# Row transforms in column pairs, a different order of the last loads, and a separated normalisation in a transformer block followed by a Fourier block

## The chip, the cores and the metric

The kernel runs on one core of one Trainium2 chip. The metric is the device time of one execution in microseconds (us); the number given is the median of several runs. A core has five engines with queues of their own: TensorE (matmuls, PE in the profile; its weight loads are PEld), VectorE (DVE), ScalarE (ACT), GpSimd (POOL) and SyncE (SP, used here only to issue DMAs). SBUF is the on-chip memory of 128 partitions, PSUM the accumulators that matmuls write, and DRAM the memory off the core.

## The reference

The input is an image of 48 x 48 tokens with 768 channels. Layer 0 is a transformer block: layer norm, 12-head attention with relative positions, a projection, and then

```python
xn2 = layernorm(x, ln2_g, ln2_b)
h = jax.nn.gelu(xn2 @ mlp_w1 + mlp_b1, approximate=False)
return x + (h @ mlp_w2 + mlp_b2)
```

Layer 1 is a Fourier block. It transforms the image in both directions, multiplies every kept frequency by two small complex layers (8 blocks of 96 channels), shrinks, transforms back and adds its input:

```python
xf = jnp.fft.rfft2(x.astype(jnp.float32), axes=(1, 2), norm='ortho')
...
y = jnp.fft.irfft2(z.reshape(B, H, Wh, C), s=(H, W), axes=(1, 2), norm='ortho')
return y.astype(x.dtype) + bias
```

All is float32. A row of 48 tokens has 25 frequencies (KW), each with a real and an imaginary part, so 50 numbers per row and channel.

## The kernel before

The 2304 tokens lie in 18 tiles of 128 partitions, x1[:, t, :], in SBUF for the whole second part of the kernel. The two edges of a 128-token tile cut rows of 48 tokens: three tiles hold 8 whole rows. Nearly all large products are made by a scheme of seven half-size products instead of eight, whose sums are made by VectorE and GpSimd.

**MLP.** It runs over three blocks p of 768 tokens (six tiles), and in each over 12 steps n of 256 hidden features. A step has hidden(p, n) in three pieces (matmuls into the PSUM banks h0 to h3, L989; VectorE sums u and c, L1001; ScalarE's gelu, L995; VectorE's sums hs, L154 to L157), and between the pieces added(p, n - 1, i) for i = 0, 1, 2, the product of the step before with the second weight matrix: seven matmuls into the banks o0 to o3, each bank emptied by VectorE into x1 or acc (L1049 to L1057). Three of the four banks are used twice within one added, so the second use waits for the first eviction.

The next block's tokens must be normalised before the block begins. normalised(p + 1, i) is written in the program in steps 4 to 9; it calls normalise (L116 to L124: two statistics, an aggregate, ScalarE's square root, a reciprocal and the tensor_scalar that writes the tile hat), and GpSimd then adds the bias b2 to x1. The order of the program holds only for TensorE here: inside manual_schedule TensorE keeps the written order, and the other engines' instructions are placed by a scheduler, which moves an instruction ahead when its inputs and its buffer are there. So the tokens of block 1 are normalised at the very beginning of block 0, and those of block 2 in the turn from block 0 to block 1. turned (L1104, L1105) transposes the six hats at the block's end.

**Forward row transform.** rows_forward(p), after each block, multiplies the block's 16 rows by the row DFT, for each half k of the channels (384 each) and each group g of three tiles (eight rows). A group gives 8 x 50 = 400 outputs, in four PSUM tiles zp of 100 partitions (two rows). Since tile edges cut rows, two of the four tiles need two matmuls: six of 128 x 100 by 384 (L1076) per group. ScalarE (or both, in the last block) copies zp to zt, and SP writes zt to DRAM, z1[k].

**Fourier part.** 14 units (7 per half, four frequencies each, the last of each half only one) go through four stages, each one round r later than the one before: columns (L1202), first (L1221 to L1238), second (L1252 to L1261) and back (yp, L1271), whose output y goes to z2 in DRAM. In a round TensorE's order is, for i = 0 to 3: back, second, first, columns, and from round 12 on one piece of the first half's inverse row transform.

**Inverse row transform.** rows_back(half, g) loads a 100 x 4 x 384 tile zo (600 KB) from z2, and makes three output tiles, each of two matmuls (rps, L1292); VectorE adds x1 (yt, L1295) and SP writes the result. zo has three buffers and yt four. In the function pieces the generators run one after the other: each load is written just ahead of its own matmuls, and the buffers decide how early it can be issued. All loads and writes are issued by SP, in one order. The second half's loads depend on the last unit's y.

## Time and profile before

| | |
|---|---|
| median of 3 runs | 2929.87 us (2922.76 to 2933.12) |
| the profiled execution's own time | 2924.9 us |
| its span, first to last instruction | 2922.9 us, TensorE clock 0.998 |
| TensorE busy | 2864.6 us (98%) |
| VectorE, ScalarE, GpSimd busy | 1791.0, 936.3, 609.8 us |
| MLP with forward row transforms | from 1625 to 2672 us |
| Fourier part and inverse row transform | from 2672 us to the end |

In a group's line of the profile, the numbers after x are the count of instructions, and after the bar the busy time in us, the mean duration of one in ns, and the idle time of the engine just before them with what ended it. In a timeline's line they are the start, the duration of the merged run, the engine, the line of the kernel, the tile written and the tiles read, the array shape of a matmul as rows x columns in use (128*100), and in brackets the idle time before. A line of the waits gives the total in us, the number of times, and the longest. A line of the chain gives start and duration of one link of the work that ended last. A float32 matmul of the program appears as two records.

### The profile page before, as it was taken

Reading aid. Unit: us, or ns where it says so; the run is one execution under the profiler, and the core shown is the slowest. Engines: PE = TensorE matmul, PEld = TensorE weight load, DVE = VectorE, ACT = ScalarE, POOL = GpSimd, SP = SyncE. Lnnn points to the kernel's source line nnn. Section 1 sums busy time; section 2 is a strip of 40 time slices with the busy share of each in tenths; the row PEclk is TensorE's granted clock in tenths of the full one; section 3 lists DMA queues with packets and bytes.
Section 4 is the critical chain, followed back from the end, with each engine's and each line's share of the span. In section 5 each row is a group of like instructions: output and inputs, shape, how many; then the busy total and the mean of one; then the engine's idle time right before and its main releaser. Section 6 shows DMA issues by size and latency. Waiting matters only on the chain. (4 is left out here: it accounts for less than half of the span.)

```text
span 2922.9 us, 40961 instructions
## 1 busy us (share of the span) xinstructions
PE 2864.6 (98%) x15659; PEld 1724.2 (59%) x15659; DVE 1791.0 (61%) x2606; ACT 936.3 (32%) x1514; POOL 609.8 (21%) x564
## 2 busy tenths in 40 slices
PE   7999999999999999999999999999999999999998
PEld 4555665555555555555555555555555555556885
DVE  5243237777777777777733666674666566665564
ACT  1011126656666565665500211122011211102331
POOL 2302110000000000000043322343332323222441
PEclk9999999999999999999999999999999999999999
DMA  3423276173462716435252111212121212113235
GB/s 127 148 88 118 92 162 123 30 135 64 82 128 41 144 34 101 109 59 87 56 177 76 43 56 53 65 64 65 57 65 54 77 54 65 54 57 99 79 93 179
DMA packets 202818, 253.03 MB, mean 87 GB/s; under 512 B 21618, under 2 KB 180978, under 8 KB 201078
## 3 DMA queue, kind: packets, MB, share of 16 engines
q1 hardware_dynamic: 202614, 250.32, 33.5%
q8 instruction: 126, 2.06, 0.3%
q14 instruction: 78, 0.64, 0.1%
HBM read 136.40 MB, written 50.14 MB: 64 GB/s over the span
## 5 line engine op out<-in xcount | busy, mean ns | idle before, releaser
L635 DVE TENSOR_TENSOR acc<-acc,main 128x768 f32<-128x768 f32 x576 | 551.9, 958 | 206.4 <-ACT main L569 149.9
L569 ACT ACTIVATE main<-sp 128x768 f32<-128x768 f32 x648 | 520.8, 812 | 138.9 <-PE sp L565 132.2
L565 PE MATMUL sp<-terms,select 64*128 64x384 f32 x1296 | 413.3, 630 | 0.0
L1051 DVE TENSOR_TENSOR main<-o,main 128x384 f32<-128x384 f32 x540 | 299.4, 557 | 40.3 <-PE o L1049 2.1
L989 PE MATMUL h<-shared,w 128*128 128x384 f32 x864 | 296.7, 486 | 0.8 <-issue 0.8
L559 PE MATMUL sp<-shared 64*128 64x384 f32 x1296 | 268.0, 490 | 2.5 <-DVE o L457 2.2
L559 PE MATMUL sp<-qT,kT 64*128 64x384 f32 x1296 | 266.7, 487 | 0.2
L612 POOL TENSOR_TENSOR inverse<-inverse,rden 128x384 f32<-128x384 f32 x36 | 46.3, 1287 | 1010.7 <-DVE rden L609 918.1
L446 PE MATMUL m<-main 128*128 128x384 f32 x756 | 247.0, 488 | 6.4 <-DVE rstd L121 3.0
L989 PEld LDWEIGHTS h<-shared,w 128*128 128x128 f32 x864 | 164.4, 190 | 116.1 <-issue 2.3
L989 PE MATMUL h<-shared,w1s 128*128 128x384 f32 x648 | 226.6, 486 | 0.0
L582 PE MATMUL op<-main,shared 128*64 128x384 f32 x1296 | 221.2, 488 | 0.0
L582 PE MATMUL op<-main,v 128*64 128x384 f32 x1296 | 219.9, 488 | 0.0
L995 ACT ACTIVATE hT<-c,vec 128x384 f32<-128x384 f32 x108 | 66.4, 615 | 466.2 <-DVE c L1001 466.1
L446 PEld LDWEIGHTS m<-main 128*128 128x128 f32 x756 | 142.6, 190 | 108.3 <-issue 8.7
L1001 DVE TENSOR_TENSOR c<-h,u 128x384 f32<-128x384 f32 x108 | 60.2, 557 | 212.3 <-PE h L989 212.3
L1049 PE MATMUL o<-w,hT 128*128 128x384 f32 x432 | 175.0, 487 | 3.0 <-DVE mv L118 2.0
L1049 PE MATMUL o<-w2s,hs 128*128 128x384 f32 x432 | 174.8, 487 | 3.1 <-DVE hs L155 3.1
L565 PEld LDWEIGHTS sp<-terms,select 64*128 64x128 f32 x1296 | 125.8, 187 | 83.9 <-issue 0.5
L989 PEld LDWEIGHTS h<-shared,w1s 128*128 128x128 f32 x648 | 123.1, 190 | 85.9
L154 POOL TENSOR_TENSOR w1s<-w 128x384 f32<-128x384 f32 x36 | 36.4, 1010 | 610.9 <-PE o L1049 289.4
L559 PEld LDWEIGHTS sp<-shared 64*128 64x128 f32 x1296 | 117.9, 187 | 61.3 <-issue 23.1
(158 smaller groups left out, 3896.8 us busy)
## 6 DMA issues: line engine op xcount, KB each, us to landing
w<-in_mlp_w_dram SPq DMA_DIRECT2D x72, 768.0 KB
terms<-col_parts SPq DMA_DIRECT2D x432, 72.0 KB
terms<-row_hi SPq DMA_DIRECT2D x216, 72.0 KB
terms<-row_lo SPq DMA_DIRECT2D x216, 72.0 KB
main<-in_qkv_w_dram SPq DMA_DIRECT2D x36, 384.0 KB
z<-zt SPq DMA_DIRECT2D x48, 150.0 KB
zo<-z SPq DMA_DIRECT2D x12, 600.0 KB
x<-in_x_dram SPq DMA_DIRECT2D x18, 384.0 KB
```

The costliest lines, as they stand in the source:

```text
L446: nc.tensor.matmul(bank, a[:, c, :], b[:, c, :], start=(first and c == 0), stop=(c == 2), skip_group_check=not first,)
L559: nc.tensor.matmul(sp[:, j, :G], kT[at, ts(kt, P)], qT[at, ts(c, G)], start=True, stop=False,)
L565: nc.tensor.matmul(sp[:, j, :G], select[at, a % 2], ready[pr, c][at, a // 2, b], start=False, stop=True,)
L569: nc.scalar.activation(p, sp[:, :, :G], AF.Exp, scale=HD**-0.5)
L582: nc.tensor.matmul(op[ts(j, 64)], v[:, kt0 + i, ts(j, 64)], ps[i][:, j, :], start=(kt0 + i == 0), stop=(kt0 + i == NT - 1),)
L612: nc.gpsimd.tensor_tensor(inverse, inverse, rden, ALU.add)
L635: nc.vector.tensor_tensor(acc, made[0] if kt == 1 else acc, p, ALU.add)
L989: nc.tensor.matmul(bank[i], a[:, c, :], b[:, c, :], start=(start and c == 0), stop=(c == 2), skip_group_check=not start,)
L995: nc.scalar.activation(h[:, i, ts(k, G)], src, AF.Gelu, bias=col(V_B1 + 2 * n + i))
L1001: nc.vector.tensor_tensor(t, src, other, ALU.add)
L1049: nc.tensor.matmul(bank[k], a, b, start=start, stop=True, skip_group_check=not start)
L1051: nc.vector.tensor_tensor(dst, bank[k], dst, ALU.add)
```

## The change

It has three parts.

1. **Rows in pairs.** In both row transforms a matmul now covers one row (64 columns of the array, 50 of them in use in the forward direction) and goes to one half of a PSUM tile's partitions; two such matmuls with different halves stand next to each other. The forward transform pads a row's 50 outputs to 64, so z1 has 64 rows per image row, zp and zt have 128 partitions, and a group takes ten matmuls of 64 columns in five pairs. The inverse writes half a tile's outputs (64 partitions) per matmul, eight in four pairs per group; its three PSUM tiles take the tags f, m and l, which the units use too. The four zt tiles of a group become slices of one tile with two buffers.
2. **Loads.** in_turn takes the place of pieces: the first half's loads run three ahead and the second half's four ahead; four of the twelve zo tiles take buffers of zt, which is free by then; the second half's loads are issued by ScalarE. The first half's pieces now stand in the rounds 13 to 16, three in each, instead of 12 to 16.
3. **Normalisation.** It is split into measured (statistics, steps 3 to 8; after the last, one square root and one reciprocal for all six tiles) and normalised (the tensor_scalar and GpSimd's addition, two tiles in each of steps 9 to 11). pinned keeps these instructions in the written order relative to their engine's other work.

```diff
-    z1 = [dram.tile([HW * 2 * KW, CH], F32, name=f"z1_{k}") for k in range(2)]
+    z1 = [dram.tile([HW * 64, CH], F32, name=f"z1_{k}") for k in range(2)]
...
-        rows = z1[half].rearrange("(r k) c -> r k c", k=KW)
+        rows = z1[half].rearrange("(r k) c -> r k c", k=32)
...
-        rows_dft = bias.tile([P, 6, 2 * 2 * KW], F32, name="rows_dft")
+        rows_dft = bias.tile([P, 3, 8, 64], F32, name="rows_dft")
...
-                    for a, parts in enumerate(((0,), (1, 2), (3, 4), (5,))):
-                        zp = psum.tile([2 * 2 * KW, CH], F32, name="zp", tag=f"o{a}")
-                        for b in parts:
+                    zp = []
+                    for pair in (((0, 0), (0, 1)), ((0, 2), (1, 3)), ((1, 2), (1, 5)),
+                                 ((1, 4), (2, 5)), ((2, 6), (2, 7))):
+                        for i, r in pair:
+                            if r // 2 == len(zp):
+                                zp.append(psum.tile([P, CH], F32, name="zp", tag=f"o{len(zp)}"))
                             nc.tensor.matmul(
-                                zp, rows_dft[:, b, :], x1[:, 3 * g + b // 2, ts(k, CH)],
-                                start=(b == parts[0]), stop=(b == parts[-1]),
+                                zp[r // 2][ts(r % 2, 64)], rows_dft[:, i, r],
+                                x1[:, 3 * g + i, ts(k, CH)],
+                                start=((i, r) not in ((1, 2), (2, 5))),
+                                stop=((i, r) not in ((0, 2), (1, 5))), skip_group_check=True,
                             )
-                        zt = turn.tile([2 * 2 * KW, CH], F32, name="zt", bufs=8)
+                    zt4 = turn.tile([P, 4, CH], F32, name="zt", bufs=2)
+                    for a in range(4):
+                        zt = zt4[:, a]
                         if p < 2:
-                            nc.scalar.copy(zt, zp)
+                            nc.scalar.copy(zt, zp[a])
                         else:
-                            balanced_copy(a, zt, zp)
-                        nc.sync.dma_start(out=z1[k][ts(4 * g + a, 4 * KW), :], in_=zt)
+                            balanced_copy(a, zt, zp[a])
+                        nc.sync.dma_start(out=z1[k][ts(4 * g + a, P), :], in_=zt)
...
+        moments = bias.tile([P, 6, 2], F32, name="moments")
+        rstd6 = bias.tile([P, 6], F32, name="rstd6")
+        pinned = tc.keep_in_program_order
+
+        def measured(p, i):
+
+            stats = upool.tile([P, 2, 6], F32, name="stats")
+            for j in range(2):
+                pinned(nc.vector.bn_stats(stats[:, j, :], x1[:, 6 * p + i, ts(j, C // 2)]))
+            pinned(nc.vector.bn_aggr(moments[:, i], stats.rearrange("p a b -> p (a b)")))
+            if i == 5:
+                pinned(nc.scalar.activation(rstd6, moments[:, :, 1], AF.Sqrt, bias=eps))
+                pinned(nc.vector.reciprocal(rstd6, rstd6))
+
         def normalised(p, i):
-
             t = 6 * p + i
             hats[i] = turn.tile([P, C], F32, name="hat2", tag="turn")
-            normalise(upool, x1[:, t, :], hats[i])
+            pinned(
+                nc.vector.tensor_scalar(
+                    hats[i], x1[:, t, :], moments[:, i, 0:1], rstd6[:, i : i + 1],
+                    ALU.subtract, ALU.mult,
+                )
+            )
             nc.gpsimd.tensor_tensor(x1[:, t, :], x1[:, t, :], b2, ALU.add)
...
-                    if p < 2 and 4 <= n < 10:
-                        normalised(p + 1, n - 4)
+                    if p < 2 and 3 <= n < 9:
+                        measured(p + 1, n - 3)
+                    elif p < 2 and n >= 9:
+                        for i in range(2):
+                            normalised(p + 1, 2 * (n - 9) + i)
...
-            zo = zin.tile([4 * KW, 4, CH], F32, name="zo", bufs=3)
-            nc.sync.dma_start(
+            if (T // G * half + g) % 5 in (1, 3):
+                zo = turn.tile([P, 4, CH], F32, name="zo2", tag="zt", bufs=2)[: 4 * KW]
+            else:
+                zo = zin.tile([4 * KW, 4, CH], F32, name="zo", bufs=3)
+            (nc.scalar if half else nc.sync).dma_start(
                 out=zo, in_=z2[half][ts(g, 16 * KW), :].rearrange("(a p) c -> p a c", a=4)
             )
             yield
-            for i in range(3):
-                yt = mid.tile([P, CH], F32, name="yt", bufs=4)
-                rp = psum.tile([P, CH], F32, name="rps", tag="f")
-                for e in range(2):
+            rp = []
+            for a, pair in enumerate(
+                (((0, 0), (0, 1)), ((1, 0), (0, 1)), ((2, 0), (1, 1)), ((2, 0), (2, 1)))
+            ):
+                if a < 3:
+                    rp.append(psum.tile([P, CH], F32, name="rps", tag="fml"[a]))
+                for i, j in pair:
+                    shared_half = (i, j) in ((0, 1), (2, 0))
                     nc.tensor.matmul(
-                        rp, irows[:, 2 * i + e, :], zo[:, i + e, :], start=(e == 0), stop=(e == 1)
+                        rp[i][ts(j, 64)], irows[:, a + i, ts(j, 64)], zo[:, a, :],
+                        start=(not shared_half or a % 2 == 0),
+                        stop=(not shared_half or a % 2 == 1), skip_group_check=shared_half,
                     )
-                nc.vector.tensor_tensor(yt, rp, x1[:, 3 * g + i, ts(half, CH)], ALU.add)
+                if a == 0:
+                    continue
+                i = a - 1
+                yt = mid.tile([P, CH], F32, name="yt", bufs=4)
+                nc.vector.tensor_tensor(yt, rp[i], x1[:, 3 * g + i, ts(half, CH)], ALU.add)
                 nc.sync.dma_start(out=out[ts(3 * g + i, P), ts(half, CH)], in_=yt)
                 yield
...
-        def pieces(gens):
-            for gen in gens:
-                yield from gen
+        def in_turn(gens, ahead):
+
+            for gen in gens[:ahead]:
+                next(gen)
+            yield
+            for g, gen in enumerate(gens):
+                for _ in range(3):
+                    next(gen)
+                    yield
+                for gen in gens[g + ahead : g + ahead + 1]:
+                    next(gen)
...
-            first_half = pieces(ends[0])
+            first_half, second_half = in_turn(ends[0], 3), in_turn(ends[1], 4)
...
-                    if r > len(units) // 2 + 4:
-                        next(first_half, None)
+                    if (r, i) == (len(units) - 2, 3) or (r > len(units) - 2 and i < 3):
+                        next(first_half)
+            next(second_half)
             for _ in first_half:
                 pass
-            for _ in pieces(ends[1]):
+            for _ in second_half:
                 pass
```

The tables that the host makes for rows_dft change their layout with it; the numbers in them are the same, with zeros in the padding.

More of the change, by code (lines that the diff above doesn't have):

```diff
@@ L1287, in rows_back @@
             yield
-            for i in range(3):
-                yt = mid.tile([P, CH], F32, name="yt", bufs=4)
-                rp = psum.tile([P, CH], F32, name="rps", tag="f")
-                for e in range(2):
-                    nc.tensor.matmul(
-                        rp, irows[:, 2 * i + e, :], zo[:, i + e, :], start=(e == 0), stop=(e == 1)
-                    )
-                nc.vector.tensor_tensor(yt, rp, x1[:, 3 * g + i, ts(half, CH)], ALU.add)
+            rp = []
[6 more added lines that the diff above has]
+                    shared_half = (i, j) in ((0, 1), (2, 0))
+                    nc.tensor.matmul(
+                        rp[i][ts(j, 64)], irows[:, a + i, ts(j, 64)], zo[:, a, :],
+                        start=(not shared_half or a % 2 == 0),
+                        stop=(not shared_half or a % 2 == 1), skip_group_check=shared_half,
+                    )
+                if a == 0:
+                    continue
+                i = a - 1
+                yt = mid.tile([P, CH], F32, name="yt", bufs=4)
+                nc.vector.tensor_tensor(yt, rp[i], x1[:, 3 * g + i, ts(half, CH)], ALU.add)
                 nc.sync.dma_start(out=out[ts(3 * g + i, P), ts(half, CH)], in_=yt)
@@ L1340, in _constants @@
             select[32 + 16 * part + w, :, :, w] = 1.0
-    fr = np.stack([cos[:, :KW], -sin[:, :KW]], 1).reshape(n, 2 * KW)
+    fr = np.zeros((n, 2, 32))
+    fr[:, 0, :KW], fr[:, 1, :KW] = cos[:, :KW], -sin[:, :KW]
     twice = np.full((KW, 1), 2.0)
@@ L1349, in _constants @@
     ir = np.concatenate([cos[:KW] * twice, -si], 0)
-    fwd = np.zeros((8 * n, 8 * 2 * KW))
+    fwd = np.zeros((8 * n, 8, 64))
     inv = np.zeros((8 * 2 * KW, 8 * n))
     for r in range(8):
-        fwd[r * n : (r + 1) * n, r * 2 * KW : (r + 1) * 2 * KW] = fr
+        fwd[r * n : (r + 1) * n, r] = fr.reshape(n, 64)
         inv[r * 2 * KW : (r + 1) * 2 * KW, r * n : (r + 1) * n] = ir
-    rows = np.zeros((P, 6, 4 * KW))
+    rows = fwd.reshape(3, P, 8, 64).transpose(1, 0, 2, 3)
     irows = np.zeros((4 * KW, 6, P))
@@ L1359, in _constants @@
         t, a = b // 2, (b + 1) // 2
-        rows[:, b] = fwd[t * P : (t + 1) * P, a * 4 * KW : (a + 1) * 4 * KW]
         irows[:, b] = inv[a * 4 * KW : (a + 1) * 4 * KW, t * P : (t + 1) * P]
```

## The prediction

> **What bounds it.** I read the page's busy shares first, then TensorE's waits from 1500 us on (nothing earlier is edited), then the row transforms and the end in the timeline, the table of stretches and the chain.
>
> ```profile
> PE 2864.6 (98%) x15659; PEld 1724.2 (59%) x15659; DVE 1791.0 (61%) x2606; ACT 936.3 (32%) x1514; POOL 609.8 (21%) x564
> ...
> PE rps L1292 <- DMA zo<-z: 5.2, 5, 1.6
> ...
> PE mp L1252 <- POOL o L1238: 3.7, 10, 0.4
> PE o L1049 <- DVE main L1051: 3.5, 5, 1.3
> PE o L1049 <- DVE hs L155: 3.1, 3, 1.1
> PE o L1049 <- DVE mv L118: 2.0, 1, 2.0
> ```
>
> TensorE is the bound: a matmul removed is time removed, and waits are a few us. The exception is the end.
>
> ```profile
> 999.86 4.04 PE L582 MATMUL op<-main,v 128*64 128x384 f32 x24
> ...
> 1965.66 15.97 PE L1076 MATMUL zp<-main,rows_dft 128*100 128x384 f32 x48
> ...
> 1755.30 0.55 DVE L156 TENSOR_TENSOR hs<-hT,hs 128x384 f32<-128x384 f32 x1
> 1756.11 0.56 DVE L1001 TENSOR_TENSOR u<-h,m 128x384 f32<-128x384 f32 x1 [0.27 <-PE h L989]
> 1756.69 0.56 DVE L1057 TENSOR_TENSOR acc<-o,acc 128x384 f32<-128x384 f32 x1
> ```
>
> A program matmul is two records here (72 row-transform matmuls, x144). The forward transform takes 15.5 us net for 24 matmuls, 0.645 us each. The attention's 64-column matmuls, in pairs on the two halves of the array's columns, take 3.97 us (to the next start, 1003.83) for 12: a pair costs 0.66 us, the price of one whole matmul. The last three lines show VectorE between two steps of the MLP: just 0.27 us idle before u.
>
> ```profile
> 2785.50:2787.50 2.00, 2.00 (x24) 2.00 (x22) 1.07 (x3) 1.05 (x4) 1.19 (x2) 1.00 0.66 235
> 2830.00:2880.66 50.66, 50.66 (x348) 39.53 (x347) 27.60 (x63) 14.68 (x42) 18.00 (x23) 1.00 0.39 119
> 2880.66:2884.00 3.34, 3.34 (x12) 1.90 (x11) 1.74 (x4) 0.00 (x0) 0.00 (x0) 1.00 0.61 197
> 2884.00:2916.00 32.00, 26.13 (x78) 14.07 (x77) 11.09 (x20) 0.00 (x0) 0.00 (x0) 1.00 0.75 239
> ...
> 2880.66 0.65 PE yp L1271 x2
> 2881.31 6.17 PE rps L1292 x20
> 2887.49 6.80 DMA zo<-z
> 2894.29 0.14 issue
> 2894.42 3.87 PE rps L1292 x12
> 2898.29 7.30 DMA zo<-z
> ```
>
> The last columns of the table are clock, DMA share and GB/s. Up to 2880.66 TensorE is full; there the last inverse column transform (yp) runs, and the remaining 42.2 us depend on its output going to memory and back: the chain alternates between 600 KB loads and their matmuls. In 2785.5 to 2787.5 practically only zo loads run, and the share is 0.66, about 10 of 16 engines.
>
> **The Trainium skill.** TensorEngine Tiling (Array Packing), Key Properties: column tiles run independently, and a change of tiling drains the array. The trace agrees: 0.66 us a pair, and the step out of the paired mode at 1003.83 costs about 0.1 us more than a matmul. DMA: Bandwidth & Descriptors, Why a DMA increments its semaphore by 16 and not by 1: a copy of 100 partitions runs on 10 engines, one of 128 on 16. The 0.66 agrees. Trainium Kernel Development and Optimization, Key Constraints: queues of several issuers share the 16 engines, so another issuer saves only issue time; nothing in this trace tests it, since before has SP alone. ScalarE: Activation LUTs, What ACT_TABLE_LOAD costs: 1283 ns and a drain; the trace has 1.28 us for each load.
>
> **Forward row transform.** 12 groups (3 blocks x 2 halves x 2), each 6 matmuls before and 5 pairs after: 12 x 1 x 0.645 = 7.7 us saved, all on TensorE's path. Evictions are four of 0.48 us (1.9 us) in a group's 3.2 us: hidden. Their DMAs grow from 150 to 192 KB but go from 10 engines to 16: hidden. The coarser zt buffer (4 slices, 2 buffers) waits for a whole group's writes, but a group lasts 3.2 us and PSUM gives nearly a group of slack: nothing; if uncovered, up to 1 us in each block. The larger rows_dft load is issued at 1624.9 and first used at 1965: nothing. The first zi loads are issued at 2666.8 and used at 2672.1; the shorter second half takes 1.3 us of that 5.3: I take 0, bounds 0 and 2.
>
> **Normalisation.** Removed: in the first block the hoisted chain stalls TensorE by 2.0 us at 1647.95 and by 0.5 after it, and in the turn from block 0 to 1 (1943 to 1964) the gaps are 4.6 us against 2.3 in the next turn, which has no such chain: 2.3 more. Saved 4.8 us, and many sub-us chains that were hidden. Added, in the changed program's order: after hs, before u, comes a measurement (two statistics and one aggregate, with starts about 1.05 us in all) in 6 steps of each of two blocks, and two tensor_scalars (about 1.9 us for a pair, as 1969.96 shows when GpSimd works too) in 3 steps. Behind them stand u and the evictions that free TensorE's PSUM banks. VectorE has 0.27 us idle there, so u is 0.8 or 1.6 us late. By the timeline, the sixth matmul of the output product reuses a bank 0.5 us after its eviction; evictions that queue run 0.47 us apart instead of 0.645 and catch up. Laid out, a measurement costs about 0.1 us (12 x 0.1 = 1.2), a pair of hats 0.8 (4 x 0.8 = 3.2), and at the block's end, where the transposes give less cover and hs is already late, 2.0 (2 x 2.0 = 4.0). The one square root per block needs two table loads (2.6 us) on ScalarE, which idles 10 us per step there; the reciprocal is placed after u and two evictions, later than the root ends: nothing. Net +3.6 us; bounds -4.8 (all hidden) and +8.
>
> **Inverse row transform until the last yp.** Before, 12 pieces (four groups) of two matmuls stand before it; after, three groups of 4 pairs: 24 x 0.645 - 12 x 0.645 = 7.7 us saved. But these matmuls were cover. Without them between steps, the second layer waits for GpSimd's o: 2.7 us from the first layer's last matmul by the timeline, under 1.8 us of work: about 0.9, and 0.3 in the next round; three steps lose their filler and wait 0.2 each as the unfilled ones do (3.7 us in 10); the single yp bank gives about 1.3 in the last rounds; rp tiles in the tags m and l, each held over a step, 0.3 three times. Drains of the paired mode are 9 x 0.1. Sum 4.9; I take 4, since some overlap. Net -3.7; bounds -7 and 0.
>
> **The end.** After the last yp (42.2 us before), 27 output writes of 192 KB and 6 loads of 600 KB remain (24 writes before). The ten shared engines then carry 6 x 0.614 + 27 x 0.197 x 10/16 = 7.0 MB at 235 GB/s: 29.8 us. Before, the same sum is 6.6 MB, 28 us, in the 32 us of 2884 to 2916: they were already about 88% used. So four loads ahead can only fill the remaining gaps. The first load still waits for the last z write (issued at 2881.9, load at 2883.9: 3.3 us after yp); meanwhile the three remaining groups of the first half run (7.7 us), about as long as a load takes. Then 4.2 us per group against 5.3 before: 3.3 + about 27 until the last load, then 2.6 us matmuls, an addition and the last write, about 5.5: 36. Saved 6 us; bounds 0 and 12 (TensorE's own 9 x 2.6 plus latency, 30 us, is the floor). ScalarE has nothing else queued behind these loads, so its waits block nobody; SP's writes no longer stand ahead of loads.
>
> **Sum.** -7.7 + 3.6 - 3.7 - 6 = -13.8 us from the profiled execution's 2924.9 us (span 2922.9 and 2.0 outside): 2911.1. The median of the three runs is 2929.9, 5 us above the profiled one; the same saving gives 2916. I say 2915.
>
> **Rivals.** *Waits take the gain.* Hats and measurements at +8, the inverse at 0 and the end at -3: with -7.7 that is -2.7, 2927. For it: 0.27 us of slack in VectorE. Against: queued evictions catch up. *More at the end.* Loads and writes interleave better than I think and the normalisation is mostly hidden: -7.7 - 2 - 6 - 11 = -27, 2903. For it: the share is only 0.75 in the last 32 us; against: ten engines bear the loads. *Slower: pairs don't overlap.* Forward pairs share their moving tile or write two banks, unlike the attention's; if their cost is 0.645 x (1 + x), the work up to the last yp grows by 0.645 x 72x = 46x us. At x = 1, -13.8 + 46 = +33, 2963. It decides from x = 0.30, a pair of 0.84 us. Against: the attention's pairs reach 0.66. *The change doesn't do what it says*: four ahead is real in the instruction order, but as the ten engines are full its effect may be nil: -7.8, 2922, counted with the first rival.
>
> **How the numbers follow.** A difference under 0.3% (8.8 us) can't be told from none. Forecast (9 to 22 us less) 0.62; more at the end 0.13; waits take the gain 0.15; slower 0.10, most of it pairs, the rest stalls beyond my bounds. Faster 0.75, same 0.15, slower 0.10. The range 2903 to 2928 is 2 to 27 us less and leaves out the pairs' case and the far ends. The likeliest case alone spans 2908 to 2921.
>
> **What would show it.** Right: zp spans of 13 us instead of 15.5 in each block, starts in pairs; TensorE waits of 0.5 to 2 us on VectorE in steps 9 to 11 of the first two blocks and none at 1648; small waits of mp on GpSimd after 2830; the last yp near 2873; groups in the end 4.2 us apart with a DMA share of 0.8. Wrong: zp at 15 us or more, or groups at 5.3 us. The prediction fails if pairs serialise, if VectorE's pinned work reaches TensorE in every step, or if loads starve the writes and so the yt buffers.

## The result and the profile after

Over 17 runs of each, the changed kernel takes 2916.08 us at the median (2906.74 to 2922.64) and the kernel before 2928.6 (2922.76 to 2939.06): a ratio of 0.996, 95% interval 0.9951 to 0.997, or 11.7 us less (8.8 to 14.4). The prediction was 2915, in a range of 2903 to 2928. The total is right; three of its four terms are not, and their errors partly cancel, so that the closeness of the sum is partly luck.

The profiled execution has a span of 2914.05 us. These are the stages of the two traces, cut at the first matmul of each (the end from the second record of the last yp to the end of the span):

| stage | before, us | after, us | change | predicted |
|---|---|---|---|---|
| up to the MLP (not edited) | 1625.2 | 1628.3 | +3.1 | |
| MLP, first block | 340.5 | 335.9 | -4.6 | |
| MLP, second block | 331.7 | 335.3 | +3.5 | |
| MLP, third block | 327.2 | 327.2 | 0.0 | |
| the three together: normalisation | | | -1.1 | +3.6 |
| three forward row transforms | 47.5 | 41.1 | -6.4 | -7.7 |
| spectral units to the last yp | 208.7 | 207.0 | -1.7 | -3.7 |
| end | 42.1 | 39.25 | -2.9 | -6.0 |
| sum from the MLP on | | | -12.0 | -13.8 |

The first line is chance: over all profiled executions here this unedited stretch took between 1625.2 and 1634.2 us. The profiled execution of before had the shortest, so the spans differ by 8.9 us only, where the stages from the MLP on differ by 12.0; the medians differ by 12.5.

The busy line of the page after:

```profile
PE 2846.6 (98%) x15803; PEld 1698.3 (58%) x15803; DVE 1774.8 (61%) x2596; ACT 929.9 (32%) x1502; POOL 613.2 (21%) x564
```

TensorE has 18 us less work and the same share. Its waits after 1500 us (total, times, longest):

```profile
PE mp L1282 <- POOL o L1268: 5.0, 13, 0.4
PE rps L1331 <- DMA zo<-z: 5.0, 4, 1.6
...
PE o L1049 <- DVE main L1051: 3.6, 3, 1.6
PE rps L1331 <- DVE yt L1340: 2.8, 3, 1.3
PE o L1049 <- DVE hs L155: 2.1, 2, 1.1
PE fp L1232 <- DMA zi<-z: 1.1, 1, 1.1
```

The wait for mv, 2.0 us, is gone. The last one, for the first frequency load, is new (before, TensorE waited 0.6 us there, for ScalarE): it is the part of the shorter second half that the prediction put at 0 with a bound of 2. TensorE's timeline at the first block's end:

```profile
1959.15 0.91 PE L1049 MATMUL o<-w,hT 128*128 128x384 f32 x2
1961.70 0.91 PE L1049 MATMUL o<-w2s,hT 128*128 128x384 f32 x2 [1.63 <-DVE main L1051]
1962.62 1.65 PE L1049 MATMUL o<-w,hs 128*128 128x384 f32 x2
1964.20 13.95 PE L1081 MATMUL zp<-main,rows_dft 128*64 128x384 f32 x80
```

The pairs overlap: 40 matmuls (80 records) take 13.88 us to the next start. A wait of 1.63 us comes shortly ahead of them, and in the third line two records take 1.65 us that took 0.81 to 0.91 elsewhere. In the trace's clock records the granted clock is 0.50 from 1962.50 to 1965.91, 3.41 us, and 1.00 around it. This is the first sign of what the prediction left out: soon after a wait, TensorE can run at half rate for a while.

The end, in stretches of 10 us (the last columns are clock, DMA share and GB/s), and then the chain of work that ended last:

```profile
2878.00:2888.00 10.00, 7.98 (x50) 3.27 (x44) 3.68 (x7) 0.00 (x0) 0.00 (x0) 1.00 0.77 253
2888.00:2898.00 10.00, 6.69 (x40) 3.10 (x40) 2.92 (x6) 0.00 (x0) 0.00 (x0) 1.00 0.81 282
2898.00:2908.00 10.00, 7.52 (x44) 2.69 (x40) 4.21 (x8) 0.00 (x0) 0.00 (x0) 1.00 0.67 244
```

```profile
2878.48 10.50 DMA zo<-z
2888.98 0.02 issue
2889.00 0.02 ACTq L1317
2889.01 0.04 issue
2889.05 7.73 DMA zo<-z
2896.78 0.14 issue
2896.92 1.53 PE rps L1331 x8
...
2899.05 5.45 DMA out_dram<-yt
...
2905.20 2.88 DMA out_dram<-yt
...
2908.19 0.57 DVE yt L1340
...
2908.78 1.83 DMA out_dram<-yt
...
2910.73 0.56 DVE yt L1340
```

The second half's first group starts at 2884.72 and its last at 2905.22, 4.1 us apart, as predicted (4.2); the share of 0.77 and 0.81 in the first 20 us is near the predicted 0.8. But the chain shows a load that is issued at the moment an earlier load lands, which isn't what "four ahead" suggests, and at the very end additions (yt) that wait for output writes to land.

### The profile page after: what moved, and what is told of

It is laid out like the page before. It is cut to its first block, busy times and chain, and to the rows that moved or that the text cites. A ratio compares the mean times of both kernels' runs of the same rounds, so it can differ in the third digit from the quotient of the medians.

```text
span 2914.0 us, 41220 instructions
## 1 busy us (share of the span) xinstructions
PE 2846.6 (98%) x15803; PEld 1698.3 (58%) x15803; DVE 1774.8 (61%) x2596; ACT 929.9 (32%) x1502; POOL 613.2 (21%) x564
```

## Experiments

### One part at a time

Three kernels each make one part of the change in the kernel before. The forward row transform alone:

```diff
-    z1 = [dram.tile([HW * 2 * KW, CH], F32, name=f"z1_{k}") for k in range(2)]
+    z1 = [dram.tile([HW * 64, CH], F32, name=f"z1_{k}") for k in range(2)]
...
+                                zp[r // 2][ts(r % 2, 64)], rows_dft[:, i, r],
+                                x1[:, 3 * g + i, ts(k, CH)],
```

> The kernel before with the forward row transform in pairs alone (its constants and the wider z1 with it). My theory: a pair of 64-column matmuls costs one whole matmul, so each of the 12 groups loses one 0.645 us: 7.7 us less in all, zp spans near 13.0 us from the first zp to the next stage, less about 1 us in the last block where the first frequency loads come late: 6.4 to 7.7 us faster, ratio 0.9974 to 0.9978. Rival, pairs do not overlap: zp spans of 28 us and 39 us slower. Rival, the row transform is bound by its evictions: spans stay at 15.5 us, no change.

Measured: 2923.25 us, ratio 0.9981 (0.9971 to 0.999), 5.6 us faster. The three zp spans are 13.67, 13.05 and 14.25 us, 6.5 less than before in all. The pairs' term of the prediction holds; what is missing to 7.7 is a little in each span for going into the paired mode and out of it (13.05 us are 20 times 0.645 and 0.15), the wait for the first frequency load in the third, and a wait of 0.4 us in the first.

The normalisation alone:

```diff
-                    if p < 2 and 4 <= n < 10:
-                        normalised(p + 1, n - 4)
+                    if p < 2 and 3 <= n < 9:
+                        measured(p + 1, n - 3)
+                    elif p < 2 and n >= 9:
+                        for i in range(2):
+                            normalised(p + 1, 2 * (n - 9) + i)
```

> The kernel before with the split and pinned normalisation alone. The prediction's theory: 4.8 us removed (2.5 in the first block's first step, 2.3 at the turn from the first block to the second), 8.4 us added: 3.6 us slower. Rival, from the stages of the two traces: the removed stall cost more than its own length, because TensorE's granted clock is low for some us after it; removed 8.7 us (first step 45.5 to 40.7 us, first turn 3.9), added 7.6: 1 us faster. In the trace the first step tells: 43.0 us if only the stall goes, 40.7 if the low clock goes with it. Steps 3 to 11 of the first two blocks 0.15 to 0.2 us longer each, the blocks' ends near 50 us.

Measured: 2927.77 us, ratio 0.9996 (0.9988 to 1.0003), 1.2 us faster by the middle of an interval that includes no change, but not 3.6 slower. The stretch from the first matmul to the third step of the first block takes 40.71 us, where it took 45.51: the rival's number. The second block's takes 40.63 in both. The numbers of the expectation's rival were read from the traces of before and after, so they are no forecast. What the normalisation adds comes out smaller here than in the changed kernel: the two blocks take 2.8 and 2.4 us more than the second block of before, where the changed kernel's take 4.1 and 3.5. Why is not shown.

The inverse row transform with its loads and buffers alone:

```diff
+            if (T // G * half + g) % 5 in (1, 3):
+                zo = turn.tile([P, 4, CH], F32, name="zo2", tag="zt", bufs=2)[: 4 * KW]
...
-            first_half = pieces(ends[0])
+            first_half, second_half = in_turn(ends[0], 3), in_turn(ends[1], 4)
```

> The kernel before with the inverse row transform in pairs, its two new tags of buffers, the loads four ahead from ScalarE's queue and the new order of the first half's pieces, but the forward transform and the normalisation as before. The prediction: 3.7 us less up to the last yp and 6 us less after it, 9.7 us faster. The stages of the two traces: 1.8 and 2.8, 4.6 us faster. If the gain at the end came from the other two parts (it should not), no change there.

Measured: 2919.48 us, ratio 0.9969 (0.9957 to 0.998). The medians differ by nearly the 9.7 us of the prediction, but the trace shows that this is chance: 1.1 us less up to the last yp, 4.9 less in the end, and 3.3 less in the first MLP block, which this kernel doesn't edit. That last number is the most useful one. The stretch holding the stall at 1648, in the kernel before and then in this one:

```profile
1650.00:1655.00 5.00, 5.00 (x13) 2.88 (x13) 2.52 (x5) 0.00 (x0) 0.00 (x0) 0.77 0.00 0
1655.00:1660.00 5.00, 5.00 (x17) 2.94 (x16) 3.41 (x7) 0.62 (x1) 0.00 (x0) 1.00 0.01 3
```

```profile
1650.00:1655.00 5.00, 3.53 (x10) 1.67 (x11) 4.92 (x13) 1.58 (x2) 2.79 (x2) 1.00 0.00 0
1655.00:1660.00 5.00, 5.00 (x17) 3.01 (x16) 2.47 (x5) 0.61 (x1) 0.00 (x0) 1.00 0.00 0
```

Both have the same stall (2.0 and 1.7 us; with the small waits around it 2.4 and 1.9). Before, the mean clock is 0.77 in the 5 us after it: the clock records have 0.50 from 1648.87 to 1652.29, 3.41 us, and matmul records start 0.64 us apart instead of 0.32 from 1649.8 to 1651.7. In the other kernel the stall, which ends at 1651.25, leaves the clock at 1.00. The stretch from the block's first matmul to its third step is 45.51 us in the one and 43.38 in the other; 40.71 without a stall. So 1.9 us of waits cost 2.7, since the two records of a matmul just after a wait start 0.40 to 0.43 us apart even at full clock, and the half rate costs about 1.7 us more, half of the 3.41. The forward part alone, with the same stall of 2.0 us and half rate from 1653.69 on, has 45.75.

The Trainium skill, TensorE: Matmul & The Clock Gate, What's actually happening, says that the clock is halved after an idle window of about 3.4 us and that this window runs freely. The traces agree on the half rate (0.64 against 0.32) and on the length: in all fourteen of them, each stretch of half rate that ends within the span lasts 3.41, 6.83 or 10.24 us, one, two or three times the same. That the place of a wait relative to such windows decides fits the two stalls above, but no run moved a stall to test it. A wait of 2.0 us was enough here, shorter than the idle window that the page gives.

The three parts alone give 5.6, 1.2 and 9.1 us, 15.9 together, and the whole change 11.7. Their intervals are wide enough for that.

### Why the inverse part gave 1.7 and not 3.7

TensorE's timeline of the changed kernel, in the last rounds:

```profile
2869.62 0.89 PE L1301 MATMUL yp<-zz,shared 96*96 96x384 f32 x2
2870.43 0.87 PE L1331 MATMUL rps<-zo,shared 100*64 100x384 f32 x4
2871.23 0.89 PE L1301 MATMUL yp<-zz,shared 96*96 96x384 f32 x2
2872.05 0.87 PE L1331 MATMUL rps<-zo,shared 100*64 100x384 f32 x4
```

From one yp to the next it is 1.61 us for a yp and a pair. Before, in the same place, two whole matmuls take 1.29:

```profile
2875.33 1.46 PE L1292 MATMUL rps<-zo,shared 100*128 100x384 f32 x4
2876.62 0.81 PE L1271 MATMUL yp<-zz,shared 96*96 96x384 f32 x2
```

A visit to the paired mode costs 0.32 us, both ways together, and there are nine of them before the last yp: 2.9 us where the prediction had 0.9. That is as much as the 2.0 us missing. The waits in this stretch came out 2.3 us longer than before (mp on GpSimd 1.3, mp on ScalarE 0.3, the last yp 0.7), less than the prediction allowed; about 0.8 of the 6.0 us by which the gain falls short of 7.7 isn't traced.

### The end: four suspects

Three profiled executions with the end of before (the kernel before, the forward part alone and the normalisation alone) have 42.1, 43.3 and 44.2 us there; four with the changed end (the changed kernel, the inverse part alone, and the kernels with the MLP work two steps earlier and with the column halves in sequence, below) have 39.25, 37.2, 39.1 and 37.8. The change is worth about 4.9 us there (means 43.2 and 38.3), and one trace is good to about 1 us. Each run below takes one or two possible limits away from the changed kernel.

**Ten engines.** Each zo load as two DMAs:

```diff
-            (nc.scalar if half else nc.sync).dma_start(
-                out=zo, in_=z2[half][ts(g, 16 * KW), :].rearrange("(a p) c -> p a c", a=4)
-            )
+            rows = z2[half][ts(g, 16 * KW), :].rearrange("(a p) c -> p a c", a=4)
+            for part in (slice(0, 96), slice(96, 100)):
+                (nc.scalar if half else nc.sync).dma_start(out=zo[part], in_=rows[part])
```

> The changed kernel with each zo load issued as two DMAs, of 96 partitions and of 4. Theory, ten of the sixteen DMA engines bear the loads and bound the end: the 96-partition part runs on all sixteen, a load alone moves near 376 GB/s where it moved 235, the 27 writes and 6 loads (9.0 MB) need 24 us where the ten engines needed 29.8, and the stretch from the last yp to the end goes from 39.6 to about 34 us (bounds 31 and 38): 5 to 6 us faster than the changed kernel, ratio to the kernel before near 0.994. Rival, latency or the four yt buffers bound the end: 39 to 40 us, ratio 0.996. Rival, twelve more DMA issues and small packets cost more than they give: over 40 us.

Measured: 2916.03 us, ratio 0.9951 (0.9934 to 0.9968), the end 40.8 us. The share rises (0.83 to 0.93 in 2880 to 2910), the time does not fall: removing the limit of ten engines, on which the prediction's 29.8 us rest, doesn't shorten the end by itself. But it isn't a clean test. By the landings in the trace, a load's large part lands 6.0 us after its issue (mean of six), where a whole load of the changed kernel takes 8.7; it is issued later, the last one 22.7 us after the first instead of 17.8. The split makes twelve transfers out of six, and what that costs is seen below, in the paragraphs on how far ahead loads are issued.

**The issuing queue.** The same loads from SP:

```diff
-            (nc.scalar if half else nc.sync).dma_start(
+            nc.sync.dma_start(
```

> The changed kernel with the second half's loads issued by SP, four ahead as they are. Theory, ScalarE's queue matters: a load that waits for its buffer on SP holds up the output writes behind it, and a write that waits for its addition holds up the loads, so the end goes back from 39.6 us towards the 42.2 of before: 2 to 3 us slower than the changed kernel, ratio to before 0.997. Rival, the order of the issues does not matter because the DMA engines or the yt buffers are the bound: no change, 0.996.

Measured: 2916.36 us, ratio 0.9955 (0.9937 to 0.9973), the end 41.3 us in its trace. On SP the first four loads do go out in 2.6 us (2877.26 to 2879.85), and the output writes suffer for it; the longest of these waits is 10.6 us:

```profile
DVE yt L1340 <- DMA out_dram<-yt: 21.4, 6, 10.6
```

The fifth and sixth load go out only 9.0 and 20.6 us after the first. The medians show no difference, but they couldn't show 2 us: the end in this trace is 2.0 us longer than the changed kernel's, as the theory had it, and whether the queue gives that is open. The Trainium skill, DMA: Bandwidth & Descriptors, Issuing engines are not separate DMA queues, says that a second issuer saves only the time to issue; the medians (2916.36 and 2916.08) are in line with it.

**How far ahead.** One load ahead instead of four:

```diff
-            first_half, second_half = in_turn(ends[0], 3), in_turn(ends[1], 4)
+            first_half, second_half = in_turn(ends[0], 3), in_turn(ends[1], 1)
```

> The changed kernel with the second half's loads from ScalarE one ahead, not four. Each load then waits in order for the group before it on TensorE only through its buffer, and ScalarE issues it at the same moment if the buffers set that moment: theory, the buffers (three and two, shared with the first half's last groups) already hold the third to sixth load back in the changed kernel, so nothing changes, end 39 to 40 us. Rival, four ahead fills the gaps as predicted: without it the groups stand 5.3 us apart and the end is 44 us or more, ratio 0.9975.

Measured: 2913.86 us, ratio 0.9954 (0.9936 to 0.9972), the end 38.0 us. The six loads go out 0, 0.6, 4.9, 11.0, 14.1 and 18.3 us after the first; in the changed kernel 0, 0.6, 5.0, 11.2, 14.3 and 17.8. So "four ahead" does nothing. The expectation named the buffers as the reason; for the fourth load that was wrong. The trace's records of the issues on ScalarE in the changed kernel, with the semaphores that each waits for and the one that it counts up:

```
2878.48  zo load 2                        counts 104
2882.85  waits for 100
2882.90  zo load 3                        counts 100
2889.00  waits for 104
2889.05  zo load 4                        counts 104
2892.09  waits for 108
2892.14  zo load 5                        counts 108
```

All transfers of SP and ScalarE take turns on eight semaphores (100 to 105, 107, 108), and each waits until the transfer that had its semaphore before has landed. Load 4 waits for load 2 to land (2888.98), loads 3 and 5 for an output write. So the depth of this prefetch is set by the turn, not by the order in the program. In the run with split loads the small parts take their turn as well, and its loads went out later for it: one small part, at 2900.21, waited for an output write that landed at 2900.19, and two large parts stood behind it.

**The four yt buffers.** The addition in place in x1:

```diff
-                yt = mid.tile([P, CH], F32, name="yt", bufs=4)
-                nc.vector.tensor_tensor(yt, rp[i], x1[:, 3 * g + i, ts(half, CH)], ALU.add)
+                yt = x1[:, 3 * g + i, ts(half, CH)]
+                nc.vector.tensor_tensor(yt, rp[i], yt, ALU.add)
```

> The changed kernel with the last addition written into x1 and the output written from there, so that the four yt buffers are gone and no addition waits for an output write. Theory, the yt buffers bound the end: VectorE waits 14.7 us for output writes there in the changed kernel; without these waits the six groups follow their loads, 30 to 34 us from the last yp to the end instead of 39.6, ratio near 0.994. Rival, the ten DMA engines of the loads bound it: VectorE's waits go and TensorE's waits for zo loads grow by as much, 39 us, ratio 0.996.

Measured: 2914.66 us, ratio 0.9944 (0.9926 to 0.9962), the end 36.8 us. Two lines of the waits, the first of the changed kernel and the second of this one:

```profile
DVE yt L1340 <- DMA out_dram<-yt: 14.7, 12, 2.5
PE rps L1331 <- DMA zo<-z: 6.6, 5, 3.1
```

VectorE's waits for output writes are gone, TensorE's for zo loads grow from 5.0 to 6.6 us, and at most 2.4 us of the end go with them. After the start of the last group 6.2 us are left instead of 8.8. That lies between theory and rival: the ratio is the theory's, the end is outside its 30 to 34, and the waits for loads grow by far less than 14.7.

**Both at once**, the addition in place and the split loads:

> As the run with the addition in place, and each zo load issued as 96 and 4 partitions. If the ten engines are the next bound once the yt buffers are gone, this is 4 to 6 us faster than the addition in place alone, the end under 30 us, ratio near 0.992. If split loads give nothing here either (as with the yt buffers), the loads are bound by their latency or by the whole of the traffic, and the ratio is that of the addition in place.

Measured: 2914.32 us, ratio 0.9948 (0.993 to 0.9966), the end 40.2 us. Its stretches (clock, share and GB/s last) say why:

```profile
2878.00:2888.00 10.00, 6.58 (x40) 2.70 (x36) 4.97 (x9) 0.00 (x0) 0.00 (x0) 1.00 0.98 315
2888.00:2898.00 10.00, 9.45 (x48) 4.79 (x48) 4.31 (x8) 0.00 (x0) 0.00 (x0) 0.83 1.01 302
2898.00:2904.00 6.00, 3.01 (x18) 1.26 (x16) 2.39 (x5) 0.00 (x0) 0.00 (x0) 1.00 0.88 270
2904.00:2914.00 10.00, 4.50 (x16) 1.78 (x16) 1.67 (x3) 0.00 (x0) 0.00 (x0) 0.79 0.28 100
```

Here all sixteen engines are full for 20 us, at 302 to 315 GB/s, nearly full for 6 more, and then mostly idle for 10, in which the last group waits for its load and runs. The large part of that load was issued only at 2898.08, 21.6 us after the first: on ScalarE it stood behind a small part that waited for its semaphore's output write to land (2897.64).

**Fewer transfers.** The addition in place, and one write of three tiles for each group but the last:

```diff
...
+                elif i == 2:
+                    nc.sync.dma_start(
+                        out=out[ds(3 * g * P, 3 * P), ts(half, CH)].rearrange("(i p) c -> p i c", p=P),
+                        in_=x1[:, ds(3 * g, 3), ts(half, CH)],
+                    )
```

> The changed kernel with the addition in place, and one output write of three tiles (576 KB) for each group but the very last, which keeps its three. Theory, the turn of the eight semaphores that all transfers of SP and ScalarE share bounds the end: in the changed kernel the fourth load is issued at the moment the second lands, because both have semaphore 104, and others wait for an output write that has theirs. With 15 transfers after the last yp where there were 33, loads wait for far fewer landings: all six are issued within about 12 us of the first (18 in the changed kernel), and the end takes 33 us (bounds 31 and 36) instead of 39.6: ratio near 0.9935. Rival, bandwidth of the ten engines bounds it: the loads are issued early but land at the same times, 37 to 39 us.

Measured: 2915.49 us, ratio 0.9948 (0.9932 to 0.9964), the end 38.3 us. The first four loads are now issued within 2.3 us, the last 13.3 us after the first: the turn of the semaphores does bind less. But the loads land no sooner (the sixth 31.3 us after the last yp, where the changed kernel has 30.0), and TensorE, which waits longer at a time for them, pays in clock:

```profile
2892.00:2896.00 4.00, 3.00 (x14) 1.56 (x16) 0.74 (x2) 0.00 (x0) 0.00 (x0) 0.80 0.82 297
2896.00:2900.00 4.00, 3.33 (x12) 1.13 (x10) 0.94 (x2) 0.00 (x0) 0.00 (x0) 0.50 0.80 299
```

The clock is 0.50 in 2896 to 2900, and the last four groups take 12.51 us in a row: 4.3 the first, at half rate, and 2.7 each of the others. The rival's 37 to 39 us is what came.

None of engines, queue, depth, buffers and number of transfers, as far as these runs take them away, sets the end: all variants lie within 36.8 and 41.3 us. What they have in common is the traffic, 9.0 MB from the landing of the last z write on. At the 302 to 315 GB/s that the sixteen engines reached when full, that is 29 us, with 3.4 ahead of it; and the last group's 2.8 us of matmuls, an addition and its writes, about 6 us, lie only partly under it. That this is the floor is argued from these numbers and not shown. A rival stands: the split loads were held up by the turn of the semaphores, and with fewer transfers, which ease the turn, each load still had only ten engines. No run has split loads and grouped writes together, nor less traffic. Which of the pairs and the two added buffers gave the 4.9 us is open too.

### Do pairs need to be neighbours?

The ten matmuls of a forward group, first all for the upper column half, then all for the lower:

```diff
...
-                    for pair in (((0, 0), (0, 1)), ((0, 2), (1, 3)), ((1, 2), (1, 5)),
-                                 ((1, 4), (2, 5)), ((2, 6), (2, 7))):
+                    for pair in (((0, 0), (0, 2), (1, 2), (1, 4), (2, 6)),
+                                 ((0, 1), (1, 3), (1, 5), (2, 5), (2, 7))):
...
```

> The changed kernel with the ten matmuls of a forward group in another order: the five for the upper half of the array's columns first, then the five for the lower. The same matmuls, banks and sums. Theory, only neighbours on different halves overlap: a group takes nine single matmuls and a half, with one overlap where the halves meet, 9 x 0.645 = 5.8 us instead of 3.2, zp spans of 23 us instead of 13, 31 us slower than the changed kernel, about 2947. Rival, a matmul of 64 columns is half as long in itself: spans stay at 13 us, no change.

Measured: 2932.03 us in one run, and in TensorE's timeline:

```profile
1966.60 18.42 PE L1079 MATMUL zp<-main,rows_dft 128*64 128x384 f32 x80
```

The three spans are 18.35, 18.95 and 18.43 us, 14.6 us over the changed kernel's, half of what was expected. A matmul of 64 columns is not half as long: order matters. But neighbours are not needed for some overlap: five matmuls of one half start 2.05 us after the five before instead of 3.2, so the other half's begin while, at 0.645 us each, nearly two are still to run.

### A better place for the normalisation

The table of the steps of the changed kernel (27.09 us each when nothing disturbs them) shows 0.15 to 0.23 us more in each step with a measurement or a pair of hats, and 49.4 us from the start of the last step to the row transform in the second block, where before had 47.3. First all of it two steps earlier:

```diff
-                    if p < 2 and 3 <= n < 9:
-                        measured(p + 1, n - 3)
-                    elif p < 2 and n >= 9:
+                    if p < 2 and 1 <= n < 7:
+                        measured(p + 1, n - 1)
+                    elif p < 2 and 7 <= n < 10:
                         for i in range(2):
-                            normalised(p + 1, 2 * (n - 9) + i)
+                            normalised(p + 1, 2 * (n - 7) + i)
```

> The changed kernel with each measurement and each pair of normalised tiles two steps of the MLP earlier (measured in steps 1 to 6, normalised in 7 to 9, where they were in 3 to 8 and 9 to 11). Theory, the pair in the last step is what makes the first two blocks' ends long: 50.1 and 49.4 us from the last full step to the row transform, where the block without any such work but with the transposes had 47.3. Moved out of it they go to 47 to 48: 3 to 5 us faster than the changed kernel, ratio near 0.9945; the 0.15 to 0.25 us of each of the nine steps stay. Rival, the ends are long because the transposes leave VectorE's evictions less cover: they stay near 49.5, ratio 0.996.

Measured: 2908.67 us, ratio 0.9924 (0.991 to 0.9938). The second block's end takes 47.37 us and its steps with such work 27.22 to 27.32: as the theory said. The pair in the last step made the ends long; the blocks are 1.8 and 1.7 us shorter, the first zp span 0.8. The timed gain over the changed kernel, 7.4 us by the medians, is more than these 4.3; the intervals allow it.

Why each step still pays is seen in VectorE's timeline, in a step of the changed kernel with a measurement:

```profile
1808.28 0.54 DVE L156 TENSOR_TENSOR hs<-hT,hs 128x384 f32<-128x384 f32 x1
1808.75 1.01 DVE L1108 BATCH_NORM_STATS2 stats<-main 128x6 f32<-128x384 f32 x2
1809.79 0.21 DVE L1109 BATCH_NORM_AGGREGATE moments<-stats 128x2 f32<-128x12 f32 x1
1809.92 0.51 DVE L1001 TENSOR_TENSOR u<-h,m 128x384 f32<-128x384 f32 x1
...
1825.98 0.56 DVE L1001 TENSOR_TENSOR c<-h,u 128x384 f32<-128x384 f32 x1 [3.31 <-PE h L989]
```

The measurement stands where VectorE is fully busy; 16 us later, in the same step, it idles for 3.31 us. The last run puts all of this work there, between the second and third part of a step, in steps 1 to 9, and has the addition in place too:

```diff
                         if n:
                             added(p, n - 1, i)
+                        if i == 1 and p < 2 and 1 <= n < 7:
+                            measured(p + 1, n - 1)
+                        elif i == 1 and p < 2 and 7 <= n < 10:
+                            for t in range(2):
+                                normalised(p + 1, 2 * (n - 7) + t)
```

> The changed kernel with each measurement and each pair of normalised tiles put between the second and the third part of its step, in steps 1 to 9 (the reciprocal with the first pair), and the last addition in place. Theory: VectorE idles 3.3 us there in every step of the third block, 0.3 us where the changed kernel has this work, so it delays nothing: steps of 27.09 us throughout, the blocks' ends at 47.3, blocks 0 and 1 at 331.7 us (before 340.5 and 331.7; two steps earlier alone 334.1 and 333.6). With 1 to 3 us from the addition in place: 2902 to 2906 us, ratio 0.9905 to 0.992. Rival, any work on VectorE between two parts reaches TensorE because the evictions behind it are late: steps of 27.2 to 27.3 us, ratio 0.9925.

```profile
1795.74 1.01 DVE L1108 BATCH_NORM_STATS2 stats<-main 128x6 f32<-128x384 f32 x2
1796.78 0.21 DVE L1109 BATCH_NORM_AGGREGATE moments<-stats 128x2 f32<-128x12 f32 x1
1799.13 0.56 DVE L1001 TENSOR_TENSOR c<-h,u 128x384 f32<-128x384 f32 x1 [2.14 <-PE h L989]
```

Measured: 2906.61 us, ratio 0.9936 (0.992 to 0.9952): the time is 0.6 us and the ratio 0.0016 above the upper ends of what was expected, while the stages are as the theory had them. The gap is 2.14 us instead of 3.31 and the work costs nothing: every step from the second on takes 27.09 us, the blocks' ends 47.38 and 47.29, the blocks 331.9 and 331.8. Its span, 2904.3 us, is the shortest of all, its median too; by the times it can't be told from the run before it in this list, and it is 14 to 23 us faster than the kernel before. Of the versions here it is the one to keep.

## Why the prediction came out right in the sum, point by point

- **Forward row transform: right, -6.4 for -7.7.** A pair costs 0.645 us. The 1.3 us are 0.15 in each of the three spans for going into the paired mode and out of it, 0.5 in the first, where half rate after the stall at the block's end takes 0.8 us (0.3 before), and 0.4 in the third, where TensorE waits 1.1 us for the first frequency load (before, 0.6 for ScalarE).
- **Normalisation, what it adds: right in the sum.** Predicted 8.4; against the second block of before the two blocks have 4.1 and 3.5, 7.6 together, of which 0.85 is half rate at the first block's end. Inside the sum two prices were off and cancelled: a measurement costs 0.15 us, not 0.1, and a pair of hats before the last step 0.2, not 0.8. The pair occupies VectorE for 1.2 us (2240.41 to 2241.59) and not 1.9, and the evictions that queue behind it do catch up: five of them take 2.82 us where they take 3.14 otherwise. What falls into the last step costs 2.1 in the second block, as put (2.0).
- **Normalisation, what it removes: wrong, 8.7 for 4.8.** The failed step is "stalls TensorE by 2.0 us at 1647.95 and by 0.5 after it", and the 2.3 of the turn: they price a stall at its own length. The first stretch lost 4.8 us (45.51 to 40.71): 2.4 of waits, 1.7 of half rate, 0.7 of slow starts. The turn lost 3.9 (51.15 against the 47.3 of the next): the timeline's idle times are 3.7 us there against 2.0 in the next turn, 1.7 more and not the 2.3 that was read, and 1.4 are half rate from 1962.90 to the row transform. Whether the clock drops differs from trace to trace: the two other kernels with the old normalisation, the forward part alone and the inverse part alone, have 45.75 and 43.38 in the first stretch and 50.27 and 49.94 in the turn, so that 8.0 and 5.4 us would go. In the traces of before and after the term is -1.1, not +3.6; how large it is on average is open.
- **Inverse row transform until the last yp: sign and mechanism right, -1.7 for -3.7.** The mis-sized term is "Drains of the paired mode are 9 x 0.1": it measured 9 x 0.32. The waits came as put, small and many: mp on GpSimd 5.0 us, after 3.7.
- **The end: right sign, -2.9 in this trace, about -4.9 over several, for -6.** The starts were right: the first group 10.3 us after the last yp, groups 4.1 us apart, the last starting after 30.8 (3.3 + 27 was put). The step that failed is what comes after it: 5.5 us were put, 8.8 came, since the last three additions wait in turn for output writes. The reason given doesn't hold as it stands: four loads ahead don't "fill the remaining gaps" (one ahead is the same), and ten engines alone don't set the end (splitting the loads gives nothing); the turn of the semaphores, which the prediction doesn't have, sets when loads are issued.
- **The rivals.** *Pairs don't overlap* fell at once: zp spans of 13 us. *Waits take the gain* and *more at the end* did not come. The nil effect of "four ahead" is true, though the end still shortened.

So the normalisation came out 4.7 us better than put, 3.9 of it in what the stalls had cost, and that made up for most of the 1.3, 2.0 and 3.1 us by which the other three gave less; the total of -12.0 is 1.8 from the -13.8. That these cancel is luck: without the low clock in before, as in the trace of the inverse part alone, 5.4 us would have been removed instead of 8.7.

## What to carry to other kernels

When you price a stall on TensorE, look at the granted clock and the matmul spacing after it: 2.4 us of waits cost 4.8 here in one trace, and 1.9 cost 2.7 in another, and so what a removed stall brings is more than its length. Put added work on an engine where its timeline idles within the same step, not merely where a share says that it is not full: in the same nine steps, the same instructions cost 1.7 us a block between two steps (333.55 us against 331.83) and nothing in the gap within the step. And a prefetch depth written in program order is worth only what the issue times in the trace show.

## What the runs showed of the hardware

- A TensorE wait of 2.0 us was followed by 3.41 us at half rate (records 0.64 us apart, not 0.32) in the kernel before, and one of 1.7 us by none in another. In the end of the run with fewer transfers, waits of 1.8 and 2.1 us took the mean clock down to 0.50 over 4 us. Half rate came in stretches of 3.41, 6.83 or 10.24 us in all traces.
- A pair of 64-column matmuls amid others costs 0.645 us and 0.32 for going into the paired mode and out of it; in a run of pairs only the 0.645 count.
- Column halves overlap without being neighbours in program order, but incompletely: 2.05 us for five matmuls that take 3.2 alone and 1.6 fully paired.
- In these kernels the transfers from SP and ScalarE share eight semaphores in turn, so that a load of 600 KB waited for the landing of another issued eight transfers before it (2888.98).
- With every engine full, mixed loads and writes with 1.5 KB packets moved 302 to 315 GB/s.
